# Two transformer blocks on one core: the first MLP for the units 0 and 1 together, the second for unit 2 alone, and unit 2's attention begun in the head

## The chip, the cores and the metric

The kernel runs on one core of a Trainium2 chip, in one launch. The metric is the device time of one execution in microseconds (us), as the median of several runs. A profiled execution gives the trace, in which the engines are PE (TensorE matmuls, with PEld for its weight loads), DVE (VectorE), ACT (ScalarE), POOL (GpSimd) and SP (SyncE, which issues all the DMA transfers here). L1044 is line 1044 of the kernel.

## The reference

The input x has 32 sequences of 64 positions and 512 channels, and everything is float32. Two blocks follow one another:

- Block 0: an RMS norm whose scale depends on a condition vector, attention with 8 query heads and one key/value head of 64 with rotary positions (`pos_ids` from an input), an output projection and a residual; then a second conditioned RMS norm and a gated MLP, `silu(h Wg) * (h Wu)` times `Wd`, with 2048 inner channels, and a residual.
- Block 1: a layer norm with conditioned scale and shift, attention with 16 query heads of 32 over 4 key/value heads that come from a latent of 128, and an output projection with a residual. With 64 positions the sparse mask hides nothing.

## The kernel before

**Units and stages.** The 2048 positions are cut into eight units of 256 (four sequences), numbered 0 to 7, held with channels on the partitions. A unit goes through `attention0` (block 0's attention, ending with the second norm, whose result stays in a tile `h2`), then the MLP, then `attention1` (the whole of block 1, which writes the unit out). `second(u)` waits until unit u's MLP is finished, runs `attention1`, and then issues `load_x(u + XB)`: there are XB = 5 buffers for x, so unit 5 is loaded when unit 0 is written out, unit 6 when unit 1 is.

**MLP by blocks.** `mlp(j)` works on the units of `BLOCKS[j]`, one or two. The matrix products are done by a Strassen-like scheme with seven products in place of eight: each weight matrix is cut into quarters, and some products need sums of quarters, of the weights as of the inputs. In a block of two units the halves of the inputs are the two units, and each matmul has 256 columns; in a block of one they are the two halves of the unit, with 128 columns. The inputs' sums are in the tile `hc`, written at the end of `attention0` of the last unit of the block (L847 to L850), as the last step behind the x-add (L679), square (L597), sum (L552, L553), mean (`ms_b`), inverse root (L564, L565) and scaling (L619).

**Weight sets.** There are 24 sets per MLP (`sequence`), for gate (m 0), up (m 1) and down (m 2) with eight q each. A set has an "f" slot of four quarters (used by the products P1, P6, P5, P7 that come first) and an "l" slot of three (P2, P3, P4). Four sets fit at a time (`MW`). The first MLP computes three sums and one more of each set from the loaded quarters (L330 to L333; sets 0 and 1 on POOL, later ones on DVE with the last on POOL) and stores them to DRAM (`kept`); the later MLPs load quarters and finished sums. In the first MLP the quarter called a21 has a tile of its own, from a pool of two, because the third place of "l" is for the last sum. `combine(n)` does the sums of set n, `done_with` stores the sums of a used set and loads set n + 4.

**Inner order of an MLP.** For each q: the first four products of gate and of up, partial sums out of PSUM (ACT copy `e` L1059, DVE L1060, L1061, L1080), the last three products (L1089), silu on ACT (L1092, L1093), and the gated products on DVE (L1098) and POOL (L1100 to L1103); after four q the `down` products. The PSUM tag "gu" has six banks; a pair's product takes two of them for gate and two for up, a single unit's one.

**What sets the order.** The head, up to the first MLP, is written out by hand: the string `FIRST` names whose next piece is issued, "a" being `attention0(0)`, "b" `attention0(1)`, "m" the modulation matrices, "i" idle matmuls, "r" a table load and "|" a mark from which on DVE may do sums of sets 2 to 4. The order of PE in it is fixed. Behind it `Order.run` takes pieces from jobs by their planned costs: the MLP of the block, the attention of the next block's units, and `chain`, which is `second(0)` to `second(5)` one after another. A block ends when its MLP and the attention of the next block's units are done. The planner writes a sequence, a scheduler in the language then sets each engine's order of instructions, and on the chip every engine runs its own list in order. The string `LAST` does the end by hand.

`angles(u)` computes the rotary angles of the units u and u + 1, 31 operations of 128 columns on DVE and two sines on ACT (L423 to L452), and then loads the next positions. In the head it runs once, for the units 2 and 3, as the end of `attention0(1)`.

Of the kernel before, what the change touches and what calls it, by code (L numbers as in the profile page):

```python
# [13 lines left out]
ALU = mybir.AluOpType  # L14
# [3 lines left out]
P = 128  # L18
# [5 lines left out]
NU = T // UT  # L24
# [23 lines left out]
STAY = 13854 + 4 * 128 + 4 * 256 + 128 + 4 * 7 * 256 + 4 * 7 * 256  # L48
FIRST = "aaaaaaa bb a mm aa bb a bbb aa b mm a bb r aa a m b a bi m b i a | b".replace(" ", "")
EARLY = 4  # L50
BLOCKS = ((0,), (1, 2), (3, 4), (5, 6), (7,))
GROUPS = ((0, 1, 2, 3), (4, 5, 6, 7))
H2 = 4
MODS = 4
# [76 lines left out]
def two_blocks(ctx: ExitStack, tc: tile.TileContext, a: dict, out: bass.AP):  # L131
# [54 lines left out]
    def work(tag, shape, name, bufs=2):  # L186
        return wk.tile(shape, F32, tag=tag, name=name, bufs=bufs)
# [76 lines left out]
    XB = 5  # L264
# [17 lines left out]
    place = {what: n for n, what in enumerate(sequence)}  # L282
    sets, odd = {"f": {}, "l": {}}, {}

# [27 lines left out]

    marks, roots = [], []

    combined = set()

    def combine(n):

        for n in range(len(combined), n + 1):
            if n not in odd:  # L320
                return
            with after(tc, mybir.EngineType.DVE, marks[0]) if 2 <= n < 5 else nullcontext():
                sums_of_set(n)
            combined.add(n)

    def sums_of_set(n):
        if sequence[n][0] == 0:
            f, l, a21 = sets["f"][n], sets["l"][n], odd[n]
            e = nc.gpsimd if n < 2 else nc.vector
            e.tensor_tensor(f[:, 0], a21, l[:, 1], ALU.add)  # L330
            e.tensor_tensor(f[:, 1], f[:, 0], f[:, 3], ALU.subtract)  # L331
            e.tensor_tensor(f[:, 2], f[:, 3], a21, ALU.subtract)
            nc.gpsimd.tensor_tensor(l[:, 2], l[:, 0], f[:, 1], ALU.subtract)  # L333

    def done_with(kind, what):
        n = place[what]
        j, m, q = what
        if j == 0:
            to = kept[3 * q + m]
            if kind == "l":  # L340
                nc.sync.dma_start(to[:, 3], sets["l"][n][:, 2])
            else:
                nc.sync.dma_start(to[:, 0:3], sets["f"][n][:, 0:3])
        if n + MW < 3 * NP:
            if kind == "l":
                load_sets(n + MW + 1)
        else:
            load_part(kind, n + MW)

# [767 lines left out]
    def down(j, g):  # L1117
# [22 lines left out]
        for q in g:  # L1140
            what = (j, 2, q)
            for i, ps in enumerate(tiles):
# [63 lines left out]
    for _ in modulation(0):  # L1206
        pass
    load_positions(2)
    load_sets(2)
    load_mod(2)  # L1210
# [29 lines left out]
    for u in range(2, XB):  # L1240
        load_x(u)
    combine(0)
# [33 lines left out]

    def in_turn(units):
        for u in units:
            while u not in x_units or u not in turned_units:
                yield 0.0, 1.0  # L1280
            late = (lambda u=u: angles(u + 2)) if u % 2 == 0 and u + 2 < NU else None
            yield from attention0(u, {"ring": "0"}, late=late)

    chain = Job(behind(), 0.8 * A1)
    for j, units in enumerate(BLOCKS):
        now = Job(mlp(j), M * len(units))
        jobs = [now, *rest]
        must = [now]
        if j == 0:
# [115 lines left out]
```

## Time and profile before

| | us |
|---|---|
| median of three runs (1020.67 to 1022.62) | 1020.71 |
| the profiled execution, its own time | 1023.49 |
| its span, from first to last instruction | 1021.7 |
| PE busy | 987.5 |
| DVE busy | 543.4 |
| POOL busy | 423.1 |
| ACT busy | 302.9 |

The span is what the views of the profile divide; the execution's own time has 1.8 us around it. PE's busy time is of matmuls that overlap at their ends, so a busy PE may still run slower than it could. Every matmul of float32 shows as two records in the trace. The granted clock of PE is given in tenths on the page and as a share in the view by stretches.

### The profile page before, as it was taken

How to read it: one execution, taken by the hardware profiler on the slowest of the kernel's cores; microseconds unless marked ns; L12 is line 12 of the kernel's file. 1: busy time of each engine (PE TensorE's matmuls, PEld its weight loads, DVE VectorE, ACT ScalarE, POOL GpSimd, SP SyncE). 2: the span in 40 equal slices, each digit the busy share in tenths (PEclk: the TensorE clock that was granted, in tenths of full speed). 3: DMA queues.
4: the chain of work that ended last, by engine and by line, in shares of the span. 5: the costliest groups of instructions: out<-in, count | busy, mean ns of one | idle time of the engine just before them, and what ended most of it. 6: DMA issues, size and time to landing. Idle time of an engine off the chain costs nothing.

```text
span 1021.7 us, 17480 instructions
## 1 busy us (share of the span) xinstructions
PE 987.5 (97%) x6710; PEld 857.6 (84%) x6710; DVE 543.4 (53%) x1188; ACT 302.9 (30%) x552; POOL 423.1 (41%) x439
## 2 busy tenths in 40 slices
PE   8999897999999999999999999999999989999998
PEld 7788887988877888888788887888788868998986
DVE  4757898654386442644446362455424632645274
ACT  4433142323215310225313351222313320425032
POOL 4336255354522433444344333554325432853252
PEclk9999998999999999999999999999999999999999
DMA  7927753724222345323242233333233424847301
GB/s 265 320 95 250 228 165 123 242 62 138 76 68 73 108 134 181 109 72 105 78 129 78 73 119 125 123 104 109 84 99 113 124 93 139 261 145 223 101 2 42
DMA packets 82642, 132.23 MB, mean 129 GB/s; under 512 B 8832, under 2 KB 48512, under 8 KB 82176
## 3 DMA queue, kind: packets, MB, share of 16 engines
q1 hardware_dynamic: 82560, 131.12, 40.1%
q8 instruction: 53, 0.87, 0.4%
q14 instruction: 29, 0.24, 0.1%
HBM read 114.31 MB, written 16.78 MB: 128 GB/s over the span
## 4 chain that ended last, share of the span: by engine, by line
PE 84%; DVE 8%; POOL 2%; DMA 2%; issue 2%; ACT 1%; POOLq 0%; SPq 0%; DVEq 0%; ACTq 0%
PE gu L1044 36%; PE down L1044 16%; PE q L623 11%; PE po L623 10%; PE sc L973 2%; PE pp L658 2%; PE kv L623 1%; PE lat L623 1%; PE cx L1003 1%; DMA stays<-in_wmlp 1%; PE cx L802 1%; ACT cT L812 1%; PE sc L781 1%; PE tab L491 1%; DVE mx L643 1%
## 5 line engine op out<-in xcount | busy, mean ns | idle before, releaser
L1044 PE MATMUL gu<-h,stays 128*128 128x256 f32 (+1 forms) x1280 | 261.2, 342 | 9.6 <-ACT gate L1092 5.8
L1044 PEld LDWEIGHTS gu<-h,stays 128*128 128x128 f32 x1280 | 208.4, 192 | 35.2 <-ACT gate L1092 6.0
L1044 PE MATMUL down<-stays 128*128 128x256 f32 (+1 forms) x1120 | 211.6, 344 | 2.0 <-DVE u_d L1060 2.0
L1044 PEld LDWEIGHTS down<-stays 128*128 128x128 f32 x1120 | 180.0, 194 | 25.9 <-issue 5.2
L1044 PE MATMUL gu<-hc,stays 128*128 128x256 f32 (+1 forms) x960 | 195.6, 339 | 0.5 <-DVE stays L331 0.5
L1044 PEld LDWEIGHTS gu<-hc,stays 128*128 128x128 f32 x960 | 157.9, 192 | 16.0 <-DVE stays L331 0.6
L623 PE MATMUL q<-h,stays 128*128 128x256 f32 x480 | 109.5, 381 | 0.0
L623 PE MATMUL po<-cT,stays 128*128 128x256 f32 x480 | 107.7, 381 | 0.9 <-ACT cT L812 0.7
L623 PEld LDWEIGHTS po<-cT,stays 128*128 128x128 f32 x480 | 90.4, 190 | 13.9 <-ACT cT L812 1.8
L623 PEld LDWEIGHTS q<-h,stays 128*128 128x128 f32 x480 | 90.6, 191 | 11.9 <-issue 0.2
L1100 POOL TENSOR_TENSOR stays<-gate,stays 128x768 f32<-128x768 f32 (+1 forms) x40 | 53.5, 1337 | 109.3 <-DVE stays L1089 102.4
L1059 ACT COPY e<-gu 128x256 f32<-128x256 f32 (+1 forms) x80 | 26.1, 326 | 193.9 <-PE gu L1044 193.8
L653 POOL TENSOR_TENSOR p<-p,sm 128x512 f32<-128x512 f32 x40 | 41.5, 1055 | 93.6 <-DVE sm L652 90.1
L634 POOL TENSOR_TENSOR qT<-u_q,v_q 128x512 f32<-128x512 f32 x30 | 38.1, 1268 | 90.0 <-DVE v_q L633 83.4
L679 DVE TENSOR_TENSOR x<-x,po 128x512 f32<-128x512 f32 x28 | 19.2, 687 | 99.2 <-PE po L623 99.2
L1060 DVE TENSOR_TENSOR u<-e,gu 128x256 f32<-128x256 f32 (+1 forms) x80 | 28.7, 360 | 61.1 <-ACT e L1059 61.1
L610 POOL TENSOR_TENSOR h<-x,stays 128x1024 f32<-128x1024 f32 x12 | 23.0, 1916 | 68.9 <-DVE x L679 51.2
L1061 DVE TENSOR_TENSOR w<-u,gu 128x256 f32<-128x256 f32 (+1 forms) x80 | 29.2, 365 | 30.9 <-PE gu L1044 30.0
L1101 POOL TENSOR_TENSOR stays<-stays 128x512 f32<-128x512 f32 (+1 forms) x40 | 43.8, 1096 | 2.7 <-DVE posf L423 0.2
L565 DVE RECIPROCAL stays<-stays 128x256 f32<-128x256 f32 (+1 forms) x23 | 35.4, 1540 | 16.9 <-ACT stays L564 16.8
L1147 POOL TENSOR_TENSOR x<-x,c 128x256 f32<-128x256 f32 x16 | 12.0, 749 | 74.8 <-DVE c L1134 74.8
L643 DVE TENSOR_REDUCE mx<-sc 128x8 f32<-128x512 f32 (+1 forms) x52 | 31.4, 641 | 17.6 <-PE sc L973 15.3
(233 smaller groups left out, 1281.9 us busy)
## 6 DMA issues: line engine op xcount, KB each, us to landing
stays<-sums SPq DMA_DIRECT2D x96, 384.0 KB, 3.1
stays<-in_wmlp SPq DMA_DIRECT2D x120, 256.0 KB, 3.1
stays<-in_wmlp SPq DMA_DIRECT2D x120, 128.0 KB, 2.6
stays<-sums SPq DMA_DIRECT2D x96, 128.0 KB, 2.4
sums<-stays SPq DMA_DIRECT2D x24, 384.0 KB, 3.7
mod<-in_mod SPq DMA_DIRECT2D x8, 512.0 KB, 5.4
x<-in_x SPq DMA_DIRECT2D x8, 512.0 KB, 5.6
a<-in_wmlp SPq DMA_DIRECT2D x24, 128.0 KB, 3.4
```

Of the source, the lines that this page charges most:

```text
L565: nc.vector.reciprocal(r, r)
L610: nc.gpsimd.tensor_tensor(by_seq(h), by_seq(x), per_seq(s, u), ALU.mult)
L623: nc.tensor.matmul(ps, w[:, k, cols], h[:, k, :], start=(k == 0), stop=(k == KC - 1))
L634: nc.gpsimd.tensor_tensor(dst, u, v, ALU.add)
L643: nc.vector.tensor_reduce(mx, s3, AX.X, ALU.max)
L653: nc.gpsimd.tensor_tensor(p8, p8, sm.unsqueeze(2).to_broadcast(wide), ALU.mult)
L1044: nc.tensor.matmul(ps[REGION[p]][:, c], w[:, slot, cols], moving, start=opening and ps.opens(p, c, k), stop=p in LATER, skip_group_check=True,
L1059: nc.scalar.copy(e, ps[0])
L1060: nc.vector.tensor_tensor(u2, e, ps[1], ALU.add)
L1061: nc.vector.tensor_tensor(w2, u2, ps[2], ALU.add)
L1100: e.tensor_tensor(act[:, 2:5], gate[:, 1:4], act[:, 2:5], ALU.mult)
L1101: e.tensor_tensor(act[:, 0:4:2], act[:, 2:4], act[:, 1:3], ALU.subtract)
```

## The change

The blocks are now (0, 1), (2), (3, 4), (5, 6), (7), and a new table `AHEAD` says whose attention is done beside which MLP: units 2, 3 and 4 beside the first, none beside the second, 5 and 6 beside the third, 7 beside the fourth. Unit 2's attention is a third stream "c" in `FIRST`, begun in the head, where "g" stands for `angles(2)`, earlier than before; the head goes on until unit 1 is through its norm. The x of unit 2 is loaded ahead of the first weight sets' successors, and there are five tiles `h2` in place of four. The quarter a21 is loaded into the third place of "l", with its two neighbours in one transfer, and the last sum overwrites it when the other sums have read it; the tile `a21` and its transfers go. Sums are stored two sets behind their making (`store`, called by `combine`), and by `done_with` where that has not come yet. Lines below the changed ones move by one to four.

```diff
-FIRST = "aaaaaaa bb a mm aa bb a bbb aa b mm a bb r aa a m b a bi m b i a | b".replace(" ", "")
+FIRST = "aaaaaaa bb a mm aa bb a bbb aa b mm a bb r aa c a g m b a bi m b i a | b bbb cc bb cc".replace(" ", "")
-BLOCKS = ((0,), (1, 2), (3, 4), (5, 6), (7,))
+BLOCKS = ((0, 1), (2,), (3, 4), (5, 6), (7,))
+AHEAD = ((2, 3, 4), (), (5, 6), (7,), ())
-H2 = 4
+H2 = 5
...
+        elif j:
+            nc.sync.dma_start(t[:, 0:2], a["wmlp"][i][:, 1:3])
+            nc.sync.dma_start(t[:, 2], kept[i][:, 3])
         else:
-            nc.sync.dma_start(t[:, 0:2], a["wmlp"][i][:, 1:3])
-            if j:
-                nc.sync.dma_start(t[:, 2], kept[i][:, 3])
+            nc.sync.dma_start(t, a["wmlp"][i][:, 1:4])
...
         for n in range(upto):
-            if n in odd:
-                continue
             load_part("f", n)
             load_part("l", n)
-            odd[n] = work("a21", [P, 2 * P], f"a21_{n}", 2)
-            nc.sync.dma_start(odd[n], a["wmlp"][3 * sequence[n][2] + sequence[n][1]][:, 3])
...
+    def store(kind, n):
+
+        if n < N0 and (kind, n) not in stored:
+            _, m, q = sequence[n]
+            stored.add((kind, n))
+            if kind == "l":
+                nc.sync.dma_start(kept[3 * q + m][:, 3], sets["l"][n][:, 2])
+            else:
+                nc.sync.dma_start(kept[3 * q + m][:, 0:3], sets["f"][n][:, 0:3])
...
-        for n in range(len(combined), n + 1):
-            if n not in odd:
-                return
-            with after(tc, mybir.EngineType.DVE, marks[0]) if 2 <= n < 5 else nullcontext():
-                sums_of_set(n)
-            combined.add(n)
+        for n in range(len(combined), min(n, N0 + 1) + 1):
+            if n < N0:
+                if n not in sets["f"] or n not in sets["l"]:
+                    return
+                with after(tc, mybir.EngineType.DVE, marks[0]) if 2 <= n < 5 else nullcontext():
+                    sums_of_set(n)
+            if n >= 2:
+                store("f", n - 2)
+                store("l", n - 2)
+            combined.append(n)
...
     def sums_of_set(n):
-        if sequence[n][0] == 0:
-            f, l, a21 = sets["f"][n], sets["l"][n], odd[n]
-            e = nc.gpsimd if n < 2 else nc.vector
-            e.tensor_tensor(f[:, 0], a21, l[:, 1], ALU.add)
-            e.tensor_tensor(f[:, 1], f[:, 0], f[:, 3], ALU.subtract)
-            e.tensor_tensor(f[:, 2], f[:, 3], a21, ALU.subtract)
-            nc.gpsimd.tensor_tensor(l[:, 2], l[:, 0], f[:, 1], ALU.subtract)
+        f, l = sets["f"][n], sets["l"][n]
+        e = nc.gpsimd if n < 2 else nc.vector
+        e.tensor_tensor(f[:, 0], l[:, 2], l[:, 1], ALU.add)
+        e.tensor_tensor(f[:, 1], f[:, 0], f[:, 3], ALU.subtract)
+        e.tensor_tensor(f[:, 2], f[:, 3], l[:, 2], ALU.subtract)
+        nc.gpsimd.tensor_tensor(l[:, 2], l[:, 0], f[:, 1], ALU.subtract)
...
     def done_with(kind, what):
         n = place[what]
...
-        if n + MW < 3 * NP:
-            if kind == "l":
-                load_sets(n + MW + 1)
-        else:
-            load_part(kind, n + MW)
+        store(kind, n)
+        load_part(kind, n + MW)
...
                     done_with("l", what)
-                    combine(place[what] + 3)
+                    combine(place[what] + 4)
...
     load_positions(2)
+    load_x(2)
     load_sets(2)
...
-    ahead = Job(attention0(1, {"ring": "1", "lean": True}, late=later_angles), A0)
+    def in_turn(units):
+        for u in units:
+            while u not in x_units or u not in turned_units:
+                yield 0.0, 1.0
+            late = (lambda u=u: angles(u + 2)) if u % 2 == 0 and u + 2 < NU else None
+            yield from attention0(u, {"ring": "0"}, late=late)
+
+    third = in_turn(AHEAD[0])
     streams = {
...
-        "b": ahead.pieces,
+        "b": attention0(1, {"ring": "1", "lean": True}),
+        "c": third,
...
+            elif name == "g":
+                later_angles()
...
-    rest = [ahead]
+    rest = []
+    for u in range(3, XB):
+        load_x(u)
...
-        if j == 0:
-            must.append(ahead)
-        if j + 1 < len(BLOCKS):
-            more = [u for u in BLOCKS[j + 1] if u > 1]
-            must.append(Job(in_turn(more), A0 * len(more)))
+        if AHEAD[j]:
+            more = third if j == 0 else in_turn(AHEAD[j])
+            must.append(Job(more, A0 * len(AHEAD[j])))
             jobs.append(must[-1])
```

More of the change, by code (lines that the diff above doesn't have):

```diff
@@ L282, in two_blocks @@
     place = {what: n for n, what in enumerate(sequence)}
-    sets, odd = {"f": {}, "l": {}}, {}
+    sets = {"f": {}, "l": {}}
     slots = {kind: [fixed([P, parts, 2 * P]) for i in range(MW)] for kind, parts in (("f", 4), ("l", 3))}
@@ L305, in load_sets @@
         for n in range(upto):
-            if n in odd:
-                continue
             load_part("f", n)
             load_part("l", n)
-            odd[n] = work("a21", [P, 2 * P], f"a21_{n}", 2)
-            nc.sync.dma_start(odd[n], a["wmlp"][3 * sequence[n][2] + sequence[n][1]][:, 3])
     marks, roots = [], []
-    combined = set()
-    def combine(n):
-        for n in range(len(combined), n + 1):
-            if n not in odd:
-                return
-            with after(tc, mybir.EngineType.DVE, marks[0]) if 2 <= n < 5 else nullcontext():
-                sums_of_set(n)
-            combined.add(n)
@@ L326, in sums_of_set @@
-    def sums_of_set(n):
-        if sequence[n][0] == 0:
-            f, l, a21 = sets["f"][n], sets["l"][n], odd[n]
-            e = nc.gpsimd if n < 2 else nc.vector
-            e.tensor_tensor(f[:, 0], a21, l[:, 1], ALU.add)
-            e.tensor_tensor(f[:, 1], f[:, 0], f[:, 3], ALU.subtract)
-            e.tensor_tensor(f[:, 2], f[:, 3], a21, ALU.subtract)
-            nc.gpsimd.tensor_tensor(l[:, 2], l[:, 0], f[:, 1], ALU.subtract)
+    combined, stored = [], set()
+    N0 = 3 * NP
+    def store(kind, n):
[6 more added lines that the diff above has]
+                nc.sync.dma_start(kept[3 * q + m][:, 0:3], sets["f"][n][:, 0:3])
@@ L335, in done_with @@
     def done_with(kind, what):
         n = place[what]
-        j, m, q = what
-        if j == 0:
-            to = kept[3 * q + m]
-            if kind == "l":
-                nc.sync.dma_start(to[:, 3], sets["l"][n][:, 2])
-            else:
-                nc.sync.dma_start(to[:, 0:3], sets["f"][n][:, 0:3])
-        if n + MW < 3 * NP:
-            if kind == "l":
-                load_sets(n + MW + 1)
-        else:
-            load_part(kind, n + MW)
+        store(kind, n)
+        load_part(kind, n + MW)
@@ L1236, in two_blocks @@
                 next(streams[name], None)
-    rest = [ahead]
+    rest = []
+    for u in range(3, XB):
+        load_x(u)
     for w, key in ((wq1, "wq1"), (wkd, "wkd"), (wkv1, "wkv1"), (wo1, "wo1")):
         nc.sync.dma_start(w, a[key])
-    for u in range(2, XB):
-        load_x(u)
     combine(0)
@@ L1275, in some @@
                 return
[L1277 to L1282, printed above, removed]
     chain = Job(behind(), 0.8 * A1)
@@ L1288, in two_blocks @@
         must = [now]
-        if j == 0:
-            must.append(ahead)
-        if j + 1 < len(BLOCKS):
-            more = [u for u in BLOCKS[j + 1] if u > 1]
-            must.append(Job(in_turn(more), A0 * len(more)))
+        if AHEAD[j]:
+            more = third if j == 0 else in_turn(AHEAD[j])
+            must.append(Job(more, A0 * len(AHEAD[j])))
             jobs.append(must[-1])
```

## The prediction

> **What bounds the kernel now.** The page first: its busy row, its granted-clock row and its chain of waits.
>
> ```profile
> PE 987.5 (97%) x6710; PEld 857.6 (84%) x6710; DVE 543.4 (53%) x1188; ACT 302.9 (30%) x552; POOL 423.1 (41%) x439
> PEclk9999998999999999999999999999999999999999
> PE 84%; DVE 8%; POOL 2%; DMA 2%; issue 2%; ACT 1%; POOLq 0%; SPq 0%; DVEq 0%; ACTq 0%
> ```
>
> TensorE sets the time: 34.2 us of the span without it, and a few slices at a lower clock, are all that an order of work can save. Next, where those lie: the view by stretches, cut at the stages that the timeline of PE shows (first MLP from 61.2, last MLP 864.3 to 963.3).
>
> ```profile
> core 0: us, PE busy (x) PEld busy (x) DVE busy (x) ACT busy (x) POOL busy (x), PEclk, DMA share, GB/s
> 53.90:61.20 7.30, 6.11 (x107) 4.61 (x106) 2.81 (x5) 4.92 (x12) 2.92 (x2) 1.00 0.01 2
> 61.20:181.80 120.60, 107.89 (x873) 100.92 (x874) 96.39 (x252) 33.85 (x66) 56.62 (x70) 0.96 0.57 187
> 181.80:864.30 682.50, 675.28 (x3916) 574.90 (x3915) 330.37 (x654) 190.51 (x317) 269.45 (x249) 1.00 0.35 108
> 864.30:963.30 99.00, 97.31 (x838) 92.31 (x838) 48.12 (x122) 33.21 (x69) 51.47 (x61) 1.00 0.64 196
> ```
>
> Idle PE is stretch less PE busy: 1.2, 12.7, 7.2 and 1.7 us. The first MLP is the bad stage, with DVE busy 80% of it (96.39 of 120.60) where the pairs' stages have 48%. Third, what PE waited for in all:
>
> ```profile
> PE pp L658 <- POOL p L653: 5.9, 9, 2.8
> PE gu L1044 <- ACT gate L1092: 5.8, 1, 5.8
> PE cx L1003 <- ACT pT L659: 2.6, 1, 2.6
> PE down L1044 <- DVE u_d L1060: 2.0, 1, 2.0
> ```
>
> The 5.8 (166.3 to 172.15) and the 2.0 (at 105.7) are both first MLP, in stretches where DVE ran `angles` between the weight sums. Fourth, the clock after such gaps, stretches of 2 us behind the 2.0 gap:
>
> ```profile
> 106.00:108.00 2.00, 0.29 (x2) 1.00 0.82 236
> 108.00:110.00 2.00, 2.00 (x15) 0.74 0.09 27
> 110.00:112.00 2.00, 2.00 (x11) 0.50 0.16 29
> ```
>
> The clock is halved for about 3.4 us. It costs: `down` x48 took 7.19 us from 107.71 against 5.4 at 0.112 each (72 in 8.04 at 864.5), so 1.6; behind the 5.8 gap the same comparison gives 2.6, behind the 2.8 gap at 832 1.5. Losses of before, idle and clock: 1.2 + (12.7+4.2) + (7.2+1.5) + 1.7 = 28.5 us.
>
> **The change, part by part.** The compiled instruction lists of both kernels hold the same work: PE, DVE and POOL have the same instructions of the same shapes (on SP 24 transfers of 128 KB are merged into others, on ACT 8 table loads fall away, 8 x 1.28 us on an engine 30% busy: nothing). Stages too are the same in kind, three pairs and two single units. So the sum is of losses only: 28.5 go, and I walk through the new lists for the new ones, pricing PE's distance between two instructions at 0.216 us for a record with 256 columns (16 in 3.45) and 0.112 with 128.
>
> Up to 53.9 PE's list is unchanged; x of unit 2 now loads ahead of two modulation matrices, which before landed about 10 us (41.9 against 32) before use: free.
>
> *Head, 53.9 to the first MLP.* The first MLP now needs unit 1 finished, so unit 1's `po` no longer hides behind MLP work. Seven `angles` operations stand on DVE ahead of unit 0's x-add: by their means (L423 to L429) about 2.8 us from 52.4, so the add ends at 55.9, not 54.6; `qs_b` waits 1.5 us (0.27 before). On ACT the square of unit 2 (1.05) stands ahead of unit 1's cT copies (1.50 for four): `cx` of its second half ends near 62.0, its copies at 63.5, and `po` waits 1.6, another 0.25 ahead of `cx`. Behind `po`: x-add 0.7, square 1.05, against `ms_a` and `tab` 1.35: 0.65. Then `q` and `kv` of unit 2 (5.2) cover by_row (1.2) and four hc operations of 0.68. Sum 4.0, from 2.5 to 7.4 with two clock drops; none of the gaps reaches 2.0, so none is charged. Start of the MLP near 81.
>
> *First MLP by a pair.* Each weight set now has 6 us of PE for its three sums (0.52 each) instead of 3; that takes the 5.8 and the 2.0 away. But DVE has, behind hc, unit 2's rotations (6.6), the second `angles` block (31 operations, about 11), softmax of unit 2 (4.2), the MLP's own 4.3 per pair of sets, and sums, some 36 us in the first 35. In its order the last read of the first `up` bank ends near 106.4, where PE wants the bank at 105.9: 0.6. On POOL the gated products (1.6+1.28+0.73+0.73) stand ahead of p (1.05): `pp` of unit 2 waits about 2.1, and the clock 1.7. Unit 3's `sc` to `pp` distance is 6.9 us as unit 2's was before, which waited 0.38 and 0.53: 1.0. For the third `angles` block and the rest of a DVE about 80% busy, 2.0: bounds 0, as in the pairs' stages, and 8, about half of the old first stage's 16.9; nearer the first, since each step has twice the PE time. Sum 7.4, range 2 to 14.
>
> *Second MLP by unit 2 alone.* It reads finished sums, as the last MLP did: 1.7 by that row.
>
> *Third MLP and the seam behind it.* x of unit 6 takes unit 1's buffer (XB is 5) and so loads only when `second(1)` is written out. Since unit 1 now ends with unit 0, and the chain of second layers starts a stage later in units, PE's list has `second(1)` end shortly before the third MLP's last `down`, and unit 6's attention run behind it with hardly any MLP left to fill. Before, unit 6 was normed 60 us of PE ahead of its MLP. Now: `sc` waits 0.5 for q; `lat` of unit 2 stands 4.0 behind `var`, which takes sqrt 0.47, recip 1.75, multiply 1.22, POOL add 1.91 and a rotation ahead of it on DVE (2.1): 1.5; `po` of unit 6 stands behind its own cT copies: 1.35. Then the seam. Unit 3 of before shows the chain alone:
>
> ```profile
> 325.03 7.07 PE L623 MATMUL po<-cT,stays 128*128 128x256 f32 x32
> 332.14 0.69 DVE L679 TENSOR_TENSOR x<-x,po 128x512 f32<-128x512 f32 x1 [2.76 <-PE po L623]
> 332.86 1.06 ACT L597 ACTIVATE sq_b<-x 128x1024 f32<-128x1024 f32 x1 [5.62 <-DVE x L679]
> 334.78 1.27 POOL L552 TENSOR_TENSOR sq_b<-sq_b 128x512 f32<-128x512 f32 x1
> 336.13 0.73 POOL L553 TENSOR_TENSOR stays<-sq_b 128x256 f32<-128x256 f32 x1
> 342.32 0.59 PE L560 MATMUL ms_b<-stays 128*128 128x256 f32 x2
> 343.45 1.75 DVE L565 RECIPROCAL stays<-stays 128x256 f32<-128x256 f32 x1
> 345.31 1.23 DVE L619 TENSOR_TENSOR h<-h,stays 128x1024 f32<-128x1024 f32 x1
> ```
>
> From the end of `po` (332.1) 4.8 us to the sum (336.86), and from `ms_b` 4.2 to h (346.54), 0.7 more to the first hc operand: 9.7. Behind unit 6's `po` PE has only `sc` of second(2) (1.1), `ms_b` and a `pp`, then the next MLP's products with hc. By the lists: 3.75 idle to `ms_b`, 2.65 to `pp`, 1.8 to T1, 0.55 to T2: 8.75. Clock 3.0, by the 2.6 behind the 5.8 gap. Sum 0.5+1.5+1.35+8.75+3.0 = 15.1, range 9 to 19.
>
> *Fourth MLP.* `lat` of unit 3 stands 5.3 behind `var`: 1.5; q to `sc` of unit 7 0.5; second(4)'s `pp` stand 6.0 and 5.0 behind `sc`, where max to p takes about 6: 1.3. Sum 3.3, range 1 to 8. *Last MLP* 1.7; behind it the lists are equal.
>
> New losses 4.0+7.4+1.7+15.1+3.3+1.7 = 33.2, against 28.5: +4.7 us. The profiled execution took 1023.49 (span 1021.7 and 1.8 around), so 1028.2; it lies 2.8 above the median of the runs, so 1025.4 there.
>
> On clock drops the row is the 2.0 us gap above, followed by half clock. The Trainium skill ("TensorE: Matmul & The Clock Gate", "Why this matters for your kernels") says that only idle gaps over some 3 us lose the clock; by that the 1.7 in the first MLP would go and the sum be +3.0.
>
> **Rivals.** *The wider first MLP saves more than the seam costs (faster).* For: pairs' stages lose about 1 us per 100 (7.2 in 682), and a pair's MLP gives each sum twice the time. With 2 in the first MLP, 2.5 in the head, 10 at the seam's stage, 1.7+1.5+1.7 elsewhere, 19.4: 1020.7 - 9.1 = 1011.6. Against: the seam's chain is fixed by its operations. It decides once the new losses stay under 28.5, that is once first MLP and head together lose under 6.7 with the others as forecast.
>
> *DVE becomes the bound of the first MLP (slower still).* For: 80% busy as before, now for some 190 us, with operations of 0.29 us that took 1.97 beside POOL (L434 at 165.28). At the old loss of 16.9: 1025.4 + 9.5 = 1034.9.
>
> *No change*: gains and seam cancel, 1020.7. That the work would not be what the words say is ruled out by the equal lists.
>
> **How the numbers follow.** Forecast 0.50, faster rival 0.25, DVE rival 0.15, no change 0.10. A measurement here can tell about 0.2%, 2.0 us, from no change. The forecast's own bounds reach across it, so faster 0.27, same 0.12, slower 0.61. The range takes in most of the faster rival and the DVE rival with a long seam: 1013 to 1040.
>
> **What would show it.** Right: in the waits of PE, no gap over 3 us between 81 and 270; a run of gaps of some 8 us together just behind unit 6's `po`, before the fourth MLP, ended by `ms_b`'s sum, p and hc, with the clock at half. Wrong: that place without a gap (then the time is below 1018), or gaps in the first MLP ended by DVE or ACT of over 8 us together (then 1034 and up), or a head that starts the MLP later than 86.

## The result, and the profile after

The changed kernel is slower: 1031.22 us as a median of four runs (1030.71 to 1032.57), beside 1021.12 for the kernel before, measured with it (1020.67 to 1022.62), ratio 1.0098 with a 95% interval from 1.0081 to 1.0116. That is +10.1 us, where +4.7 was forecast. The profiled execution has a span of 1030.8.

The page of the kernel after, its busy row, its granted-clock row and its chain of work:

```profile
PE 985.8 (96%) x6710; PEld 852.6 (83%) x6710; DVE 558.4 (54%) x1188; ACT 293.0 (28%) x544; POOL 419.5 (41%) x439
PEclk9989999999999999999999999899999999999999
PE 78%; DVE 14%; POOL 3%; issue 2%; DMA 2%; ACT 1%; SPq 0%; POOLq 0%; DVEq 0%; ACTq 0%
```

Two things stand out. DVE holds 14% of the chain where it held 8%. And DVE is busy 15 us longer (558.4 for 543.4) with the same 1188 instructions, while POOL is busy no longer than before: DVE's operations have become slower, not more.

The kernel after, cut at the stages that the timeline of PE shows: head from 53.90, first MLP of the units 0 and 1 from 84.87, MLP of unit 2 from 306.85, MLP of 3 and 4 from 402.50, MLP of 5 and 6 with the seam ahead of it from 624.70, MLP of unit 7 from 865.50.

```profile
core 0: us, PE busy (x) PEld busy (x) DVE busy (x) ACT busy (x) POOL busy (x), PEclk, DMA share, GB/s
53.90:84.87 30.97, 24.66 (x187) 20.38 (x186) 25.16 (x52) 11.28 (x21) 7.88 (x7) 0.89 0.09 35
84.87:306.85 221.98, 206.53 (x1159) 174.16 (x1158) 153.99 (x311) 57.66 (x93) 91.17 (x88) 0.98 0.33 111
306.85:402.50 95.65, 93.98 (x821) 89.62 (x820) 45.93 (x119) 27.91 (x61) 46.28 (x57) 1.00 0.70 223
402.50:624.70 222.20, 221.21 (x1274) 189.24 (x1272) 98.80 (x200) 54.59 (x94) 87.12 (x84) 1.00 0.37 115
624.70:865.50 240.80, 231.90 (x1369) 194.02 (x1368) 114.57 (x215) 66.16 (x114) 91.72 (x84) 0.98 0.31 97
865.50:977.20 111.70, 111.12 (x942) 105.01 (x941) 52.17 (x133) 35.12 (x74) 53.02 (x64) 1.00 0.56 179
```

Stretch less PE busy gives idle PE: 6.3, 15.5, 1.7, 1.0, 8.9 and 0.6 us. The bad stages are the first MLP, then the seam, then the head. What PE waited for in the whole run (seven of the rows; each has the total, the number of waits and the longest):

```profile
PE gu L1046 <- DVE gate L1091: 7.6, 2, 4.6
PE ms_b L562 <- POOL stays L555: 3.8, 2, 3.3
PE po L625 <- ACT cT L814: 3.7, 4, 1.6
PE row_b L493 <- DVE stays L436: 2.8, 1, 2.8
PE gu L1046 <- DVE hc L849: 2.0, 1, 2.0
PE qs_b L574 <- ACT sq_b L599: 1.7, 2, 1.1
PE gu L1046 <- DVE stays L1091: 1.5, 1, 1.5
```

The rows with L1091 are the first MLP, the one with L436 the head, and in both PE waited for DVE. In the first MLP it waited for the partial sums of `gate`, which stood in DVE's list behind parts of an `angles` block (gaps of 4.56 at 113.85 and 3.00 at 243.87). The rows with `ms_b` and `hc` are the seam. There the timeline of PE has what the forecast had drawn, a row of gaps just behind unit 6's `po`:

```profile
633.63 1.67 PE L625 MATMUL po<-cT,stays 128*128 128x256 f32 x7
635.23 1.58 PE L975 MATMUL sc<-kb,qT 64*64 64x128 f32 x32
640.16 1.22 PE L562 MATMUL ms_b<-stays 128*128 128x256 f32 x2 [3.35 <-POOL stays L555]
643.18 1.11 PE L660 MATMUL pp<-stays,p 128*128 128x128 f32 x4 [1.80 <-POOL p L655]
646.26 4.22 PE L1046 MATMUL gu<-hc,stays 128*128 128x256 f32 x8 [1.96 <-DVE hc L849]
```

Now the rows that explain the first MLP. Timeline of DVE in the kernel after, from 106.85, and below it POOL in the same stretch:

```profile
106.85 0.41 DVE L1100 TENSOR_TENSOR stays<-gate,gu 128x256 f32<-128x256 f32 x1
107.18 1.59 DVE L447 SCALAR_TENSOR_TENSOR stays<-stays 128x128 f32<-128x128 f32 x1
108.80 1.31 DVE L448 SCALAR_TENSOR_TENSOR stays<-stays 128x128 f32<-128x128 f32 x1
110.15 0.70 DVE L435 TENSOR_SCALAR stays<-stays 128x128 f32<-128x128 f32 x1
110.89 0.83 DVE L436 TENSOR_TENSOR stays<-stays 128x128 f32<-128x128 f32 x1
```

```profile
107.08 1.54 POOL L1102 TENSOR_TENSOR stays<-gate,stays 128x768 f32<-128x768 f32 x1 [4.67 <-DVE stays L1091]
108.70 1.27 POOL L1103 TENSOR_TENSOR stays<-stays 128x512 f32<-128x512 f32 x1
110.05 0.73 POOL L1104 TENSOR_TENSOR stays<-stays 128x256 f32<-128x256 f32 x1
110.85 0.72 POOL L1105 TENSOR_TENSOR stays<-stays 128x256 f32<-128x256 f32 x1
```

Four small angle operations, 0.22 to 0.29 each where they run alone, took 4.43 us together, and each ended 0.07 to 0.15 us behind the end of a POOL operation (108.77 behind 108.62, 110.11 behind 109.97, 110.85 behind 110.78, 111.72 behind 111.57). They did not run slowly; they waited for POOL. Operations with an input in PSUM do not: `u` of L1062 with 256 columns took 0.42 in the 22 cases that began beside a POOL operation and 0.41 in the 26 others.

The angle operations waited as much in the kernel before, though: all 105 of them took 42.8 us there and 42.5 here. What has grown are the sums of weight sets that DVE does, first before, then after:

```profile
L330 DVE TENSOR_TENSOR stays<-a,stays 128x256 f32<-128x256 f32 x22 | 12.0, 546 | 8.2 <-DMA stays<-in_wmlp 8.2
L332 DVE TENSOR_TENSOR stays<-stays,a 128x256 f32<-128x256 f32 x22 | 11.6, 526 | 3.7 <-DMA a<-in_wmlp 2.2 <-issue 1.5
L331 DVE TENSOR_TENSOR stays<-stays 128x256 f32<-128x256 f32 x22 | 10.8, 492 | 0.1
```

```profile
L344 DVE TENSOR_TENSOR stays<-stays 128x256 f32<-128x256 f32 x22 | 16.7, 761 | 0.0
L343 DVE TENSOR_TENSOR stays<-stays 128x256 f32<-128x256 f32 x22 | 15.6, 711 | 0.0
L342 DVE TENSOR_TENSOR stays<-stays 128x256 f32<-128x256 f32 x22 | 14.5, 661 | 11.9 <-DMA stays<-in_wmlp 11.9
```

That is 34.4 us before and 46.8 after, 12.4 of DVE's 15. Of the 66 sums 32 now began beside a POOL operation and took 1.02 on average; before, it was 24 of them and 0.70. The others took 0.42 in both kernels.

### The profile page after: what moved, and what is told of

Its sections match the earlier page's. It is cut to its first block, busy times and chain, and to the rows that moved or that the text cites. A ratio compares the mean times of both kernels' runs of the same rounds, so it can differ in the third digit from the quotient of the medians.

```text
span 1030.8 us, 17415 instructions
## 1 busy us (share of the span) xinstructions
PE 985.8 (96%) x6710; PEld 852.6 (83%) x6710; DVE 558.4 (54%) x1188; ACT 293.0 (28%) x544; POOL 419.5 (41%) x439
## 4 chain that ended last, share of the span: by engine, by line
PE 78%; DVE 14%; POOL 3%; issue 2%; DMA 2%; ACT 1%; SPq 0%; POOLq 0%; DVEq 0%; ACTq 0%
PE gu L1046 32%; PE down L1046 16%; PE po L625 10%; PE q L625 9%; PE pp L660 1%; PE lat L625 1%; PE sc L975 1%; PE kv L625 1%; PE cx L804 1%; DMA stays<-in_wmlp 1%; DVE stays L567 1%; PE cx L1005 1%; DVE stays L343 1%; DVE stays L344 1%; DVE sm L653 1%
## 5 line engine op out<-in xcount | busy, mean ns | idle before, releaser
L1046 PE MATMUL down<-stays 128*128 128x256 f32 (+1 forms) x1120 | 208.9, 339 | 1.0 <-POOL stays L1103 1.0
L1046 PE MATMUL gu<-hc,stays 128*128 128x256 f32 (+1 forms) x960 | 197.8, 342 | 11.1 <-DVE gate L1091 7.6
L1046 PEld LDWEIGHTS down<-stays 128*128 128x128 f32 x1120 | 176.7, 190 | 23.4 <-issue 2.9
L1046 PEld LDWEIGHTS gu<-hc,stays 128*128 128x128 f32 x960 | 158.5, 192 | 28.5 <-DVE gate L1091 8.4
L625 PE MATMUL po<-cT,stays 128*128 128x256 f32 x480 | 110.1, 387 | 3.7 <-ACT cT L814 3.7
L1062 DVE TENSOR_TENSOR u<-e,gu 128x256 f32<-128x256 f32 (+1 forms) x80 | 28.9, 361 | 79.1 <-ACT e L1061 78.9
L567 DVE RECIPROCAL stays<-stays 128x256 f32<-128x256 f32 (+1 forms) x23 | 35.4, 1540 | 23.1 <-ACT stays L566 23.1
L1091 DVE TENSOR_TENSOR gate<-gu,u 128x512 f32<-128x512 f32 (+1 forms) x40 | 23.2, 581 | 37.7 <-PE gu L1046 37.2
L1091 DVE TENSOR_TENSOR stays<-gu,u 128x512 f32<-128x512 f32 (+1 forms) x40 | 23.2, 581 | 33.4 <-PE gu L1046 33.2
```

The costliest lines, as they stand in the source:

```text
L567: nc.vector.reciprocal(r, r)
L625: nc.tensor.matmul(ps, w[:, k, cols], h[:, k, :], start=(k == 0), stop=(k == KC - 1))
L1046: nc.tensor.matmul(ps[REGION[p]][:, c], w[:, slot, cols], moving, start=opening and ps.opens(p, c, k), stop=p in LATER, skip_group_check=True,
L1062: nc.vector.tensor_tensor(u2, e, ps[1], ALU.add)
L1091: nc.vector.tensor_tensor(c12_21, ps.late_pair()[:, :, 0], u2.to_broadcast([P, 2, ht]), ALU.add)
```

## The experiments

The kernel before was measured again beside every group of runs, with medians of 1021.1 to 1023.0, so kernels are set against each other by their ratios to it; 0.001 is 1.0 us. By the 95% intervals a difference of under about 2 us means nothing.

**1 and 2. Most of the angle arithmetic left out, in both kernels.** In `angles` only 6 of 35 operations of a block stay, the cast, a sign, the product with `freq`, one rounding (two operations) and the last product:

```diff
-        nc.vector.tensor_scalar(sign, sign, 2.0, -1.0, ALU.mult, ALU.add)
-        nc.vector.tensor_tensor(posf, posf, sign, ALU.mult)
...
-        fraction(hi, lo)
-        nc.scalar.activation(acc, hi, AF.Sin, scale=TWO_PI)
+        fraction(prod, ang)
+        nc.scalar.activation(acc, prod, AF.Sin, scale=TWO_PI)
```

For the changed kernel:

> The changed kernel with most of the arithmetic of `angles` left out (6 of 35 DVE operations a block stay; the angle tables of units 2 to 7 are not the reference's). Theory A, the angle blocks on DVE make the gaps of the head and of the first MLP: the gaps of 1.67, 4.56, 1.24, 1.50 and 3.00 in the first MLP (12.0) go with 3.7 of half clock behind them, and in the head the 2.84 ahead of row_b with most of its 2.8 of half clock: 14 to 19 us less, so 1012 to 1017. Rival B, the weight sums and the MLP's own operations crowd DVE: only the head's part goes, 4 to 6 us less, 1025 to 1027.

Measured 1015.18, ratio 0.9936 (0.9917 to 0.9956), 16 us less than the changed kernel: theory A. The first MLP's idle time fell from 15.5 to 6.4; in the head the gap of 2.84 and the half clock went; the seam stayed as it was (3.34, 1.80 and 1.96). For the kernel before:

> The kernel before with the same cut of `angles` (the angle tables of units 2 to 7 are not the reference's). Theory A: the gaps of 5.84 and 2.02 go with 4.1 of half clock behind them, and some of the smaller ones: 10 to 13 us less, 1008 to 1011; the changed kernel stays 3 to 8 us slower under the same cut, by its seam. Rival B, the three sums every 3 us of TensorE's time are the old stage's limit: under 4 us less, 1017 or more, and the changed kernel is then the faster one under the cut.

Measured 1008.54, ratio 0.9873 (0.9849 to 0.9896), 13 us less. Here the first MLP's idle time fell from 12.7 to 8.4, and its half clock went. So in both kernels a good part of the first MLP's losses hangs on the angle blocks, more of it in the changed kernel, and the order of units did not free the first MLP of them. Without them the change costs 0.63% still, 6.4 us, which the seam and the storing part (3, 9 and 10) are large enough to explain.

**3. The chain of second layers with a larger share.**

```diff
-        chain.total = 0.8 * A1 * (len(BLOCKS[j - 1]) if j else 1)
+        chain.total = 1.4 * A1 * (len(BLOCKS[j - 1]) if j else 1)
```

> The changed kernel with the chain of second layers given a larger share in the order (1.4 for 0.8), so that second(1) ends earlier, x of unit 6 loads earlier, and unit 6's attention is done with 40 instructions of the third MLP's products still to come. The forecast's reason for the seam (nothing left to fill behind unit 6's po): the gaps of 3.35, 1.80 and 1.96 and 1.5 of half clock go, 7 to 10 us less, 1021 to 1024. Rival: the chain's waits only move to another place, under 3 us less.

Measured 1022.04, ratio 1.0005 (0.9990 to 1.0019), 9.5 us less, as the forecast's reason for the seam says. The first MLP kept its gaps (4.56 and 3.00), so the gain is not from there. Of the waits of PE between 600 and 660 only one row is left in that kernel, of a kind that the kernel before has too (2.77 at 832):

```profile
PE pp L660 <- POOL p L655: 3.9, 4, 2.8
```

**4. The angle block in 12 DVE operations for 35**, the way `first_angles` does it: the five products on ACT into one tile of 640 columns, which DVE rounds, subtracts and sums in one operation each.

```diff
+        for k, (piece, turn) in enumerate(((hi, 0), (hi, 1), (hi, 2), (lo, 0), (lo, 1))):
+            nc.scalar.mul(prods[:, k], piece, TURN[turn])
+        nc.vector.tensor_scalar(rnds, prods, ROUND, ROUND, ALU.add, ALU.subtract)
+        nc.vector.tensor_tensor(prods, prods, rnds, ALU.subtract)
+        nc.vector.tensor_reduce(acc, prods.rearrange("p k c -> p c k"), AX.X, ALU.add)
```

> The changed kernel with `angles` written with 12 DVE operations a block for 35 (five products on ACT into one tile, rounded, subtracted and summed together). Nothing of the computation is left out. Theory A: most of what the cut of the arithmetic gives, 9 to 15 us less, 1016 to 1022. Rival B: within 4 us of the changed kernel; or worse, if the 10 more operations on ACT delay the copies and silu: 1033 or more.

Measured 1026.74, ratio 1.0048 (1.0031 to 1.0064), 5 us less, below the expected 9 to 15. The first MLP did become 9.9 us shorter: its idle time fell from 15.5 to 8.6, with no half clock left in it. The head gave some 2 us of that back (the first MLP begins at 86.87, not 84.87), since the ten ACT operations of a block now stood among copies that PE needs there; the rest is open. (The head's own angle operations and the blocks now also share one tile.) The waits of PE in the head of that kernel:

```profile
PE cx L797 <- ACT pT L654: 3.2, 1, 3.2
PE row_b L486 <- DVE stays L447: 2.2, 1, 2.2
```

**5. The first MLP's gated products on DVE instead of POOL.** This gives the busier engine more to do, and takes away the POOL operations that its angle operations and weight sums waited for.

```diff
-        e = nc.gpsimd
+        e = nc.gpsimd if j else nc.vector
```

> The changed kernel with the four gated products of each set of the first MLP on DVE instead of POOL. Theory C, an operation of DVE with both operands in SBUF waits for the end of a running POOL operation: between 107.1 and 111.6 four angle operations took 4.43 us instead of 1.03; the products on DVE cost about 2.5 a set (0.42 at 256 columns, 0.68 at 512, 0.95 at 768) and free as much of this, so the first MLP is as before or shorter: 1026 to 1033. Rival D, only DVE's own busy time counts: 2.5 more in each of the three or four sets beside an angle block, and new gaps in the others: 8 us or more slower, 1039 up.

Measured 1021.46, ratio 0.9999 (0.9983 to 1.0014), 10 us less, beyond what theory C expected and against theory D. The gap of 4.56 became 0.95, that of 3.00 became 0.35, and the first MLP has no half clock any more. Its row by stretch, to be set against the row 84.87:306.85 above:

```profile
83.30:295.10 211.80, 203.72 (x1159) 172.36 (x1159) 150.74 (x343) 57.86 (x93) 56.77 (x56) 1.00 0.35 116
```

DVE has 32 instructions more (343 for 311) and is busy 3 us less (150.74 for 153.99): more went in waits behind POOL than the products cost. The weight sums take 35.0 us for 46.9 and the angle operations 35.2 for 42.5. Two operations of the angle block, the largest product, and the `gate` sums that end the wait at 113.29 in that kernel:

```profile
105.67 0.95 DVE L1102 TENSOR_TENSOR stays<-gate,stays 128x768 f32<-128x768 f32 x1
106.54 0.29 DVE L447 SCALAR_TENSOR_TENSOR stays<-stays 128x128 f32<-128x128 f32 x1
112.56 0.68 DVE L1091 TENSOR_TENSOR gate<-gu,u 128x512 f32<-128x512 f32 x1
113.49 0.28 DVE L448 SCALAR_TENSOR_TENSOR stays<-stays 128x128 f32<-128x128 f32 x1
```

The rows show one thing more. The scheduler has set DVE's list anew: L448 and the two operations behind it stood ahead of the `gate` sums in the changed kernel (these began at 117.68) and stand behind them here, and it is the same at the gap of 3.00. So the 10 us are of shorter waits and of a better order together, and no run parts the two.

**6. The same move in the kernel before.**

> The kernel before with the gated products of the first MLP on DVE instead of POOL. If the same wait of DVE behind POOL made the old first MLP's gaps of 5.84 and 2.02 (one angle operation at 165.28 took 1.97): most of the two and of the 4.1 of half clock go, 6 to 10 us less, 1012 to 1016, and the change keeps its distance of some 9 us. If the old gaps came of three sums every 3 us and the products only load DVE more: 1022 or slower.

Measured 1022.22, ratio 0.9990 (0.9978 to 1.0001): no change that can be told from noise, where 6 to 10 us less were expected. The gap of 2.02 went, the 5.84 stayed at 5.99. Timeline of POOL and of DVE in that kernel, ahead of the gap that ends at 166.73:

```profile
160.16 1.91 POOL L610 TENSOR_TENSOR h<-x,stays 128x1024 f32<-128x1024 f32 x1 [5.37 <-DVE x L679]
162.03 1.58 POOL L552 TENSOR_TENSOR sq_b<-sq_b 128x512 f32<-128x512 f32 x1
```

```profile
160.53 1.96 DVE L1100 TENSOR_TENSOR stays<-gate,stays 128x384 f32<-128x384 f32 x1
162.41 1.34 DVE L434 TENSOR_TENSOR stays<-stays 128x128 f32<-128x128 f32 x1
```

The wait is the same, the partner another: there POOL runs the products and sums of a norm, and now a gated product that DVE has taken over waits for them. Without the move that stretch had L434 at 165.28 with its 1.97 beside L610. Which POOL operations stand beside the angle block is what has to be looked up, not that POOL is busy.

**7. The head's angle block behind unit 1's last piece.** In `FIRST`:

```diff
-aa c a g m b a bi m b i a | b bbb cc bb cc
+aa c a m b a bi m b i a | g b bbb cc bb cc
```

> The changed kernel with the angle block of units 2 and 3 put behind unit 1's last head piece instead of ahead of unit 0's `po`. If the head's loss is what stands ahead of unit 0's x-add and reciprocal on DVE: the gaps of 1.12 and 2.84 shrink to about 0.3 and 0.8 and the 2.8 of half clock goes, 3 to 6 us less, 1025 to 1028. Rival: the tables of unit 2 now wait for a block of some 12 us that begins near 62, so 2 us or more at `tab` (74.7), and the time is that of the changed kernel within 2 us or above.

Measured 1035.87, ratio 1.0131 (1.0116 to 1.0146), 3 us slower: the rival. The gap of 1.12 fell to 0.33 and the 2.84 went, but the tables of unit 2 now wait:

```profile
PE tab L493 <- DVE stays L454: 7.3, 1, 7.3
```

**8. The head's angle block earlier**, behind unit 0's scores:

```diff
-aaaaaaa bb a mm aa bb a bbb aa b mm a bb r aa c a g m b
+aaaaaaa bb a mm aa bb a g bbb aa b mm a bb r aa c a m b
```

> The changed kernel with the angle block of units 2 and 3 emitted earlier in the head, behind unit 0's scores, so that its 35 DVE operations stand among unit 0's softmax and unit 1's rotations and all ahead of unit 0's x-add. If the head's loss is the block between x-add and the reciprocal of unit 0, stretched by POOL's products: the gaps of 1.12 and 2.84 go with the half clock behind them, 4 to 6 us less, 1025 to 1027. Rival: any place in the head costs the same, since DVE is as full there (the rotations and the softmax of units 0 and 1 come later): 1029 to 1033.

Measured 1030.42, ratio 1.0079 (1.0052 to 1.0106): the rival again, 2 us less at best. The wait goes to unit 1's value transposes:

```profile
46.44 0.68 PE L764 MATMUL vt<-stays,vT 64*128 64x64 f32 x4 [4.23 <-DVE vT L747]
```

In the three places tried, the 35 operations cost PE about the same or more. DVE is busy 25.16 of 30.97 us in the head, 81%: as far as these places show, what the head loses by is the block in it, not where in it.

**9 and 10. The storing part alone, done and undone.** On the kernel before only the sets' new handling (`load_part`, `store`, `combine`, `sums_of_set` and `done_with` as in the diff of the change):

```diff
-            odd[n] = work("a21", [P, 2 * P], f"a21_{n}", 2)
...
+            nc.sync.dma_start(t, a["wmlp"][i][:, 1:4])
...
-                    combine(place[what] + 3)
+                    combine(place[what] + 4)
```

> The kernel before with the storing part of the change alone: the spare quarter is loaded into the last sum's place (24 transfers of 128 KB merged into others), sums and stores as in the changed kernel, blocks and order of units as before. The prediction's price is nothing: 1018 to 1024. Rival: the last sum overwrites a quarter that is read late, and sets start later: the first MLP's gaps grow, 1027 or more.

Measured 1026.47, ratio 1.0038 (1.0023 to 1.0053): 3.9 us slower, neither nothing nor the rival. On the changed kernel the same diff taken back, with blocks and order of units left as changed:

> The changed kernel with the storing part undone: the spare quarter in a tile of its own again, sums and stores as in the kernel before, blocks and order of units as changed. By the prediction's price, nothing: 1029 to 1033. By the 3.9 us that the storing part alone cost on the kernel before: 1025 to 1029.

Measured 1029.07, ratio 1.0059 (1.0040 to 1.0078): 4.0 us less than the changed kernel. Two runs agree that this part, priced at nothing, costs about 4 us, but their profiles do not agree on where. With the old handling PE idles 10.7 us in the changed kernel's first MLP, against 15.5 with the new; no gap can be named as the storing part's, since with another order of DVE's list the gaps stand at other places. On the kernel before, idle PE is the same with the new handling as without (34.0 and 34.2 us of the span), and the longer time is PE's busy time (990.7 for 987.5), with one stretch of half clock more, at 309.

**11 and 12. What in the storing part.** With the sums three sets ahead again:

```diff
-                    combine(place[what] + 4)
+                    combine(place[what] + 3)
```

> The changed kernel in which the sums of a set are emitted three sets ahead, as before the change, and not four (DVE's list differs by some 70 moved rows, SP's list is the same). If the storing part's 4 us come from where the four-ahead sums stand in DVE's list: 1027 to 1029. If they come from anything else (the stores, the shared place of spare quarter and last sum): 1030 to 1033.

Measured 1031.70, ratio 1.0081 (1.0062 to 1.0101). With the stores when a set is used up:

```diff
-            if n >= 2:
-                store("f", n - 2)
-                store("l", n - 2)
```

> The changed kernel in which a set's sums are stored when the set is used up, as before the change, and not two sets after they were made (SP's list differs). If the 4 us come from the early stores, which stand on SP ahead of later loads: 1027 to 1029. Otherwise 1030 to 1033; if the load of the next set then waits for the later store: 1034 or more.

Measured 1032.36, ratio 1.0084 (1.0068 to 1.0100). Both lie within 2 us of the changed kernel, 1.7 and 1.4 less, so neither alone is all of it; that the two add up was not tried. What is left besides is the shared place of the spare quarter and the last sum, which ties each set's sums to one another, and `done_with`, which now loads the next "f" as soon as its slot is free and not together with "l". Neither was tried by itself, and the cause of these 4 us stays open.

**13 to 16. Cures together**, by the diffs shown. The chain's share (3), the short blocks (4) and the head's block behind "|" (7):

> The changed kernel with the larger share for the chain, the angle block with 12 DVE operations, and the first of these blocks behind unit 1's last head piece. Nothing of the computation is left out. If the three losses are separate: 9 less by the chain, 9 to 10 less in the first MLP, 4 to 6 less in the head, 1031.2 - 23 = 1008, range 1004 to 1013. If one gives back what another takes (the tables of unit 2 late, or the chain's waits on a fuller DVE): 1014 to 1020.

Measured 1011.28, ratio 0.9891 (0.9876 to 0.9906): faster than both kernels, 3 us above the 1008 expected and inside its range. Its waits in the head are 1.72 at `tab`, 1.45 at qs_b and 2.23 at unit 1's `po`. With the gated products on DVE too (5):

> The kernel with the three cures (chain's share, 12 DVE operations for the angles, the first block later) and the first MLP's gated products on DVE too. Nothing of the computation is left out. If the gaps left there (2.70 at 103.6, 1.63 at 119.5) are still waits of DVE behind POOL: 2 to 5 us less than the 1011.3 without the move, 1006 to 1009. If with short angle blocks there is little left to free: 1010 to 1015.

Measured 1010.75, ratio 0.9881 (0.9865 to 0.9897): the second case, little was left to free (gaps of 2.70 and 1.01), and not to be told from the run without the move. The same, with the head's block earlier (8 for 7):

> The kernel with the chain's larger share, the 12-operation angle blocks, the first MLP's gated products on DVE, and the first angle block at the same earlier place in the head instead of behind unit 1's last piece. Nothing of the computation is left out. The gaps of 1.72 at `tab` and 1.47 at qs_b and the 3.4 us of half clock there go: 2 to 5 us less than 1010.8, 1006 to 1009. Rival: its ten ACT operations delay the copies of units 0 and 1: 1010 to 1014.

Measured 1014.44, ratio 0.9920 (0.9900 to 0.9940): 4 us slower than that, the rival; its waits of PE in the head are 3.8 for row_b, 2.6 for a modulation row on ACT and 2.4 for qs_b. And the kernel before with short blocks and the products on DVE (4 and 5):

> The kernel before with the angle blocks of 12 DVE operations and the first MLP's gated products on DVE. Nothing of the computation is left out. If the angle blocks beside POOL were what the old first MLP lost (16.9), 10 to 14 of it go: 1007 to 1012, as good as the changed kernel with its cures, so that the new order of units brings nothing by itself. Otherwise 1015 or more.

Measured 1017.17, ratio 0.9945 (0.9926 to 0.9964), 6 us less and the second case expected (1015 or more). The new order of units with these two cures, a chain that finishes earlier and the head's block behind "|" (run 14) is then 6 us ahead of the old order with the two cures alone. Whether the old order would gain by a larger share of the chain was not tried, so how much of the 6 us is the order's stays open. Of the kernels that leave nothing out, the fastest are those of runs 13 and 14, some 12 us below the kernel before.

## Why the prediction was right or wrong

Direction and place were right, the size was not: +10.1 where +4.7 was forecast.

| term | forecast, us | measured, us |
|---|---|---|
| head | 4.0 | 6.3 idle and 2.7 of clock |
| first MLP, units 0 and 1 | 7.4 | 15.5 idle and 3.3 of clock |
| MLP of unit 2 | 1.7 | 1.7 |
| MLP of 3 and 4, seam, MLP of 5 and 6 | 15.1 + 3.3 | 1.0 + 8.9 idle and 3.5 of clock |
| last MLP | 1.7 | 0.6 |
| storing part | 0 | about 4, spread over these rows |

Clock costs here are the longer operations: 32 instructions of unit 1's `po` in 9.85 us for 7.17; in the first MLP the two stretches of 3.4 us at half clock behind the gaps of 4.56 and 3.00; at the seam `ms_b` in 1.22 for 0.59, four `pp` in 1.11 for 0.60 and eight products with `hc` in 4.22 for 1.89.

**First MLP, the step that failed.** Two terms of its sum were mis-sized: the 0.6 for the stretch with the second `angles` block, where the gap of 4.56 came, and the "2.0 for the third `angles` block and the rest of a DVE about 80% busy", where gaps of 1.50 and 3.00 came. Together PE waited 9.1 us for L1091, for 2.6 forecast. The DVE work was priced by mean durations from the kernel before, as some 36 us in 35, and in the new order the same operations took longer: the weight sums 0.71 each for 0.52, since more of them met a POOL operation and each then waited longer. An angle block was too low from the start: it has 35 operations, not 31, and took 14.2 us (42.5 for three), not about 11, of which a third is waiting, since 21 of the 105 operations began beside a POOL operation and took 0.98 on average, the others 0.26. The waits of `pp` that the sum put at 2.1 there did not come. Taking the gated products away from POOL took 10 us off, about the size of the error, though by a new order of DVE's list as well.

The row that told this stood in the prediction, L434 at 165.28 with 1.97 us, as an argument for the rival of DVE as a bound; that rival's mechanism came true, and its price for this stage, the old loss of 16.9, was nearer to the measured 18.8 than the 7.4.

The Trainium skill has the rule ("SBUF — State Buffer", "Who interferes with whom"): DVE shares one pair of its SBUF ports with GpSimd and needs it for an instruction with two inputs in SBUF, or for a copy, cast or `tensor_scalar` in a two-port mode; the pair is locked, and the one that comes second is blocked. The rows agree with it: angle operations and weight sums waited (weight sums 1.02 beside POOL against 0.42), those with an input in PSUM did not (L1062: 0.42 against 0.41), and `tensor_reduce`, which the page says never contends, kept 0.68.

**Head.** The gaps that were forecast came (1.12 and 1.60 for 1.5 and 1.6), the first by the mechanism named, DVE's block ahead of unit 0's x-add. The second is the four copies of `cT` that follow `cx` and nothing else: ACT had waited 3.76 us for `cx` and was long done with the square of unit 2. Two things were left out: the rest of the block behind the x-add, which stands ahead of unit 0's reciprocal and which POOL's norm products stretched too, and the clock. Rows of DVE and of ACT in the kernel after (ahead of the last row of each fence some are left out):

```profile
54.22 1.09 DVE L440 TENSOR_SCALAR stays<-stays 128x128 f32<-128x128 f32 x1
55.34 1.84 DVE L435 TENSOR_SCALAR stays<-stays 128x128 f32<-128x128 f32 x1
57.22 0.29 DVE L436 TENSOR_TENSOR stays<-stays 128x128 f32<-128x128 f32 x1
57.55 1.18 DVE L440 TENSOR_SCALAR stays<-stays 128x128 f32<-128x128 f32 x1
60.62 0.55 DVE L567 RECIPROCAL stays<-stays 128x64 f32<-128x64 f32 x1
```

```profile
56.02 0.31 ACT L566 ACTIVATE stays<-qs_b,stays 128x64 f32<-128x64 f32 x1
63.03 1.50 ACT L814 COPY cT<-cx 64x256 f32<-64x256 f32 x4 [3.76 <-PE cx L804]
```

The reciprocal (L567), which ends the wait at this place in the kernel before, had its input from ACT at 56.33 and began at 60.62. That is the 2.84 gap at row_b, which was not in the sum, and the half clock behind it, which the sum put at nothing because no single forecast gap reached 2.0. "Head starts the MLP later than 86" did not happen (84.87), though it came near.

**Seam.** Right, and its cause is shown by run 3. Gaps of 3.35, 1.80 and 1.96 stand for the 3.75, 2.65, 1.8 and 0.55 that were forecast, `po` of unit 6 waited 1.27 for 1.35, `lat` 0.46 for 1.5. The half clock (10.2 us long) lay over gaps for 3.8 us and cost 3.5 by the rows, for 3.0 forecast.

**Fourth and last MLP.** The waits of `lat`, `q` and `pp` that I read out of distances in PE's list hardly came: 3.3 and 1.7 were too much. In the total they hid about 4 us of the 11 by which the first MLP's term was short.

**The storing part.** "24 transfers merged: nothing" looked at transfers alone. The part also moves the sums in DVE's list, and the prediction went by the lists of the whole change, where that can't be seen apart.

**What the rows do not close.** Idle and clock by the table are about 43.5 us against 28.5 before, 15 more, while the span grew by 9.1. (In the 28.5 the clock behind the 2.0 gap is 1.6; 7.19 less 5.4 is 1.8.) Over the whole span idle PE grew by 10.8 us and busy PE fell by 1.7, so the kernel before spent busy time that is not in its 28.5. Some of it is in `sc` groups: of those with 32 instructions two took 1.58 and 1.32 for the usual 1.10, and of those with 64 two took 1.67 and 1.55 for 1.16; in the kernel after one took 1.58. The rest was not found.

**The rivals.** No gap over 3 us between 81 and 270 was to show the forecast right; there was one of 4.56. DVE gaps there of over 8 us together were to show the DVE rival; they were 9.1 by the rows with L1091, though the time that was to go with them, 1034 and up, did not come. So the case that happened is the forecast's seam and the DVE rival's first MLP at once. The faster rival's condition (head and first MLP together under 6.7) was missed by far, but the kernel of run 13, at 1011.28, shows that the new order can reach the 1011.6 of that rival once its losses are cured.

## What to carry to other kernels

An operation's mean duration is a price only with its neighbours: before small DVE operations on SBUF are moved, look which POOL operations they will lie beside, and price each meeting at what is left of the POOL operation. A change with two parts should be compared part by part, in lists too; the part that was priced as merged transfers alone cost about 4 of the 10 us. And moving work onto the busier engine can shorten that engine's busy time, if it takes away what it waits for.

## What the runs showed of the hardware

DVE's waits behind POOL are written into its durations, not into its idle time: a stretched operation looks busy. 20 of the 21 angle operations in the kernel after that began beside a POOL operation ended 0.08 to 0.09 us (`TENSOR_SCALAR` and the cast) or 0.15 us (with two tensor inputs) behind its end. `RECIPROCAL`, with its input in SBUF, did not wait: 1.75 us for 256 columns in the 11 cases beside POOL and in the 8 others.

The same wait need not cost the same clock: the gap of 2.57 at `cx` stands in the kernel before and in the one with the storing part alone, both times ahead of operations that start at 308.5 and 308.7. In the first the clock stayed at 1.00 (`down` x6 behind it in 1.56), in the second it fell to 0.50 (2.87). Kernels that differ by a few us can differ by one such stretch, some 1.5 us, without any other cause that the rows show. Executions of one kernel differ in this too: the ten of run 3 took 1020.2 to 1025.7 us, the three above 1024 with a mean granted clock of 0.988, the others with 0.992 or 0.993.
